# Three sets of operand buffers that change roles, a reordered outer sum and a third small buffer in an attention and feed-forward kernel

## The chip, the cores and the metric

The kernel runs on one core of a Trainium2 chip. The metric is the device time in microseconds of one execution. A core has a matrix engine (TensorE, PE in the profile; PEld is its loading of weights), a vector engine (VectorE, DVE), a scalar engine (ScalarE, ACT), a general engine (GpSimd, POOL) and a queue that starts transfers (SyncE, SP). Each works through its own list of instructions in order and waits on semaphores for the others.

## The reference

The input has 8 batches of 512 rows of 512 numbers, all in float32. The first part is an attention layer with low-rank projections and rotary positions. The second part, which the change is about, is a feed-forward layer with Hadamard transforms:

```python
x = x + _layernorm(attention(_layernorm(x)))        # first part
h = _layernorm(x)
h = fwht(h * SU_ug) / 64                            # transform over 512
up   = h @ W_up.T   * (Wscale_ug[:2048] * 64)       # 512 -> 2048
gate = h @ W_gate.T * (Wscale_ug[2048:] * 64)
g = silu(gate) * up
g = fwht(g * SU_dp) / 64                            # transform over 2048
y = g @ W_down.T * (Wscale_dp * 64)                 # 2048 -> 512
x = x + _layernorm(y)
```

The second transform is folded into `W_down` beforehand, on the chip.

## The kernel before

**Two stages.** The attention stage takes the first 900 us or so. The feed-forward stage takes the 8 batches in four pairs (p = 0 to 3); batches 2p and 2p + 1 are pair p. Each pair runs 8 blocks (i = 0 to 7); a block makes 128 of the 2048 inner columns twice over, i and i + 8, for both batches, for gate and up.

**Seven products instead of eight.** The four quarters of weights (i and i + 8, two halves of the 512 inputs) and the four quarters of the transformed input (two batches, two halves) are multiplied as a 2 by 2 block product in a Strassen-like form: seven products, numbered and ordered by `ORDER = (1, 2, 6, 5, 7, 3, 4)`. Products 1, 2 and 3 use quarters of the input as they are (B11, B21, B22). Products 5, 6, 7 and 4 use T1, T2, T3 and T4, which VectorE makes by four subtractions in `operand` (L230): T1 = B12 - B11, T2 = B22 - T1, T3 = B22 - B12, T4 = B21 - T2.

**First half** (pair 0). `seven` (L1153) runs the seven products for gate and then for up of each block; a pass over one of them is a unit, u = 0 to 15. During the units the layer's inputs of the next pair are brought in by `in_step` (L177): `in_flip` transposes 128 rows on TensorE and VectorE writes `xflat` (L197); `in_had` multiplies it with a Hadamard matrix (L204), and copies (L209) and adds (L210 to L214) write it to the pair's input tile `xb[b]`. `FIRST_CUTS` says how many steps a unit takes: none to two, all in `middle`, after product 3. `hook(n)` is called after product n and, in the last unit, makes operands for pair 1.

**Second half** (pairs 1 to 3). The same scheme is used once more inside each product: gate and up, and the two halves of the product's operand, make a second 2 by 2 product, so `deep` (L1102) makes each of the seven products out of seven small ones, 128 x 256 matmuls (L1112) into one of four PSUM banks. Their operands are three subtractions each, `tt` (`deep_operand`, L1005), and one in place (`deep_last`, L1010). What follows one product's small ones:

```python
nc.scalar.copy(m1, small(1))                    # L1119 ACT
nc.vector.tensor_add(gate[:, :HS], small(2), m1)    # L1120
nc.vector.tensor_add(u2, small(6), m1)          # L1122
nc.scalar.copy(m5, small(5))                    # L1123 ACT
nc.vector.tensor_add(u3, small(7), u2)          # L1126
nc.gpsimd.tensor_add(up[:, HS:], u3, m5)        # L1127
nc.vector.tensor_add(gate[:, HS:], small(3), u2)    # L1128
nc.gpsimd.tensor_add(gate[:, HS:], gate[:, HS:], m5)    # L1129
nc.vector.tensor_add(up[:, :HS], small(4), u3)  # L1131
```

`m1` and `u2` are halves of one tile, `m5` and `u3` of another; four tiles of the tag "sig" go round, so each kind has two. `gate` and `up` are halves of a `pr` tile; six `pr` tiles go round. `pair` (L1325) then lets GpSimd combine the seven `pr` tiles (L1334, two instructions for each sum), ScalarE applies silu (L1151) and VectorE scales (L1147), and the result `g` goes into the down-projection's queue.

**What orders the work.** The order is written out by hand. `place(n, at)` is called inside product n at at = 1, 2, 3, and there the queue's down-projection matmuls (L1212), the norms and stores of finished batches, and the operands of the next pair are put in. `prepare` (L1287) has a table with keys (i, n, at): "T" makes a T, "tt" one of a product's three subtractions, "last" the one in place. For the next pair it starts in block NH - 2 = 6 of the pair before and ends in block 0 of the pair itself.

**Buffers of the operands.** Input tiles `xb[b]` of all pairs go round in two buffers of tag kT and two of tag qT. T1 to T4 of all pairs lie in the two tiles of `home`. The weights of the last batch's down-projection (`wd_load_last`, L1078) take new tiles of the tags kT, qT and xT.

Of the kernel before, what the change touches and what calls it, by code (L numbers as in the profile page):

```python
# [33 lines left out]
def sandwich_kernel(  # L34
# [164 lines left out]
    def in_had(j):  # L199
        b, t = rows[j]  # L200
        if t == 0:
            xb[b] = qkv.tile([P, NK, S], F32, tag=("kT", "qT")[b % 2], name=f"xb_{b}")
        ps = room["bank"](f"fxh_{j}").rearrange("p (k q) -> p k q", k=NK)
        nc.tensor.matmul(ps, lhsT=h128, rhs=xflat[j], start=True, stop=True)  # L204
        z, a = room["z"](f"xz_{j}"), room["a"](f"xa_{j}")
        pv_ = ps.rearrange("p (a t) q -> p a t q", t=2)
        zv = z.rearrange("p (a t) q -> p a t q", t=2)[:, :, 1, :]
        av = a.rearrange("p (a t) q -> p a t q", t=2)
        nc.scalar.copy(zv, pv_[:, :, 1, :])  # L209
        nc.vector.tensor_add(av[:, :, 0, :], pv_[:, :, 0, :], zv)  # L210
        nc.vector.tensor_sub(av[:, :, 1, :], pv_[:, :, 0, :], zv)
        d = xb[b][:, :, ts(t, P)]
        nc.gpsimd.tensor_add(d[:, 0:2, :], a[:, 0:2, :], a[:, 2:4, :])
        nc.gpsimd.tensor_sub(d[:, 2:4, :], a[:, 0:2, :], a[:, 2:4, :])  # L214
# [4 lines left out]
    def operand(p, k):  # L219

        b11, b21 = xb[2 * p][:, 0:2], xb[2 * p][:, 2:4]
        b12, b22 = xb[2 * p + 1][:, 0:2], xb[2 * p + 1][:, 2:4]
        if k == 0:
            ops[p] = {"B11": b11, "B21": b21, "B22": b22}
        o = ops[p]
        if p == 0 and k < 2:
            home.append(qkv.tile([P, NT, D], F32, tag="v", name=f"T{k + 1}"))
        o[f"T{k + 1}"] = home[k % 2][:, 2 * (k // 2) : 2 * (k // 2) + 2]
        a, b = [(b12, b11), (b22, o.get("T1")), (b22, b12), (b21, o.get("T2"))][k]
        nc.vector.tensor_sub(o[f"T{k + 1}"], a, b)  # L230

# [846 lines left out]
    def wd_load_last():  # L1078
        n = len(wd_last)
        if n % 4 == 0:  # L1080
            pool, tag = [(qkv, "kT"), (qkv, "qT"), (xt_p, "xT"), (xt_p, "xT")][n // 4]
            wd_home.append(pool.tile([P, NT, D], F32, tag=tag, name=f"wdl_{n // 4}"))
        wd_last.append(wd_home[-1][:, n % 4])
        nc.sync.dma_start(out=wd_last[n], in_=wdd[:, ts(order_of(NB - 1)[n], D)])

# [7 lines left out]
    def product(p, i, what, n):  # L1093
# [5 lines left out]
            )  # L1099
        return ps  # L1100

    def deep(p, i, n, gate, up, copied, place):  # L1102

        x_, t, w = ops[p][OPERAND[n]], tt[p, n], wq.pop((p, i, n))
        rhs = {
            1: x_[:, 0, :HS], 2: x_[:, 1, :HS], 6: t[:, 1], 5: t[:, 0],
            7: x_[:, 0, HS:], 3: x_[:, 1, HS:], 4: t[:, 2],
        }

        def small(m):  # L1110
            ps = ubank(f"d{n}{m}_{p}_{i}")[:, :HS]
            nc.tensor.matmul(ps, lhsT=w[:, INNER[m]], rhs=rhs[m], start=True, stop=True)  # L1112
            return ps

        one, two = (
            fs.tile([P, 2, HS], F32, tag="sig", name=f"d{k}{n}_{p}_{i}", bufs=4) for k in "ab"
        )
        m1, u2, m5, u3 = one[:, 0], one[:, 1], two[:, 0], two[:, 1]
        nc.scalar.copy(m1, small(1))  # L1119
        nc.vector.tensor_add(gate[:, :HS], small(2), m1)  # L1120
        place(1)
        nc.vector.tensor_add(u2, small(6), m1)  # L1122
        nc.scalar.copy(m5, small(5))  # L1123
        copied()
        place(2)
# [4 lines that stand above are left out]
        place(3)  # L1130
        nc.vector.tensor_add(up[:, :HS], small(4), u3)  # L1131
# [155 lines left out]
    def prepare(p, i, n, at):  # L1287
        q = p + 1 if i >= NH - 2 else p
        if q >= NP or q == 0:
            return  # L1290
        todo = {
            (NH - 2, 1, 2): [("ops",), ("tt", 1, 0)], (NH - 2, 1, 3): [("tt", 1, 1)],
            (NH - 2, 2, 3): [("tt", 1, 2)], (NH - 2, 3, 1): [("tt", 2, 0)],
            (NH - 2, 3, 2): [("tt", 2, 1)], (NH - 2, 3, 3): [("tt", 2, 2)],
            (NH - 1, 7, 2): [("T", 0)], (NH - 1, 7, 3): [("T", 1)], (NH - 1, 3, 1): [("last", 1)],
            (NH - 1, 3, 2): [("T", 2)], (NH - 1, 4, 1): [("tt", 6, 0)],
            (NH - 1, 4, 2): [("tt", 6, 1)], (NH - 1, 4, 3): [("tt", 6, 2)],
            (0, 1, 1): [("T", 3)], (0, 1, 2): [("last", 2)], (0, 1, 3): [("last", 6)],
            (0, 2, 1): [("tt", 5, 0)], (0, 2, 3): [("tt", 5, 1)], (0, 6, 1): [("tt", 5, 2)],
            (0, 6, 2): [("last", 5), ("tt", 7, 0)], (0, 5, 1): [("tt", 7, 1)],  # L1300
            (0, 5, 2): [("tt", 7, 2)], (0, 5, 3): [("last", 7)], (0, 7, 1): [("tt", 3, 0)],
            (0, 7, 2): [("tt", 3, 1)], (0, 7, 3): [("tt", 3, 2)], (0, 3, 1): [("last", 3)],
            (0, 3, 2): [("tt", 4, 0)], (0, 3, 3): [("tt", 4, 1)], (0, 4, 1): [("tt", 4, 2)],
            (0, 4, 2): [("last", 4)],
        }
        for kind in todo.get((i, n, at), ()):
            make(q, *kind)
# [12 lines left out]


    PARTS = {1: (1, 3), 2: (1, 3), 6: (1, 2, 3), 5: (1, 3), 7: (1, 3), 3: (1, 2, 3), 4: (1, 3)}
    rest_of = {}

    def pair(p, i, inputs):  # L1325

        bA, bB = 2 * p, 2 * p + 1
        pr = {}
        before = dict(rest_of)
        rest_of.clear()  # L1330

# [56 lines left out]
        for n in ORDER:  # L1388
# [4 lines left out]
            if n in (2, 5, 3):  # L1393
                if inputs:
                    step(n, *inputs.pop(0))
            pr[n] = pr_tile(f"pr{n}_{p}_{i}")
            deep(
                p, i, n, pr[n][:, 0], pr[n][:, 1], lambda n=n: copied(n), lambda at, n=n: place(n, at)
            )
            if n == 2 and i == 0:  # L1400
                add(2, 2, 1)
            elif n == 6:
                add(6, 6, 1)
            elif n == 7:
                add(7, 7, 6)
                add(6, 6, 5)
                add(5, 5, 7)
            elif n == 3:
                add(3, 3, 6)
            elif n == 4:  # L1410
                add(4, 4, 7)
        rest_of.update(c22=(pr[5], bB, i + NH), c12=(pr[3], bB, i), c21=(pr[4], bA, i + NH))

# [5 lines left out]
    for u, (p, i, what) in enumerate(units):  # L1421
# [24 lines left out]
        def hook(n):  # L1446
            if sums and n != 1:
                sums.pop(0)()
            if u == 2 and n in (1, 2):
                in_stats(first + n - 1)  # L1450
            if u == 2 * NH - 1:
                for kind in {
                    1: [("ops",), ("tt", 1)], 2: [("tt", 2)], 5: [("T", 0)], 7: [("T", 1), ("last", 1)],
                    3: [("T", 2)], 4: [("tt", 6)],
                }[n]:
                    make(1, *kind)

        seven(p, i, what, filler, middle, hook)
        if u == 1:
# [129 lines left out]
```

## Time and profile before

| what | us |
|---|---|
| median of three runs | 2120.41 |
| the three runs | 2116.99, 2121.7, 2120.41 |
| the profiled execution's own time | 2117.1 |
| its span | 2115.3 |
| TensorE busy in it | 2081.0 |
| GpSimd busy | 1573.5 |
| VectorE busy | 1408.2 |
| ScalarE busy | 745.3 |

The profile is of one execution. Busy times overlap, since the engines work side by side. The granted clock of TensorE was 0.998 of full speed over the span. A line of a groups view has the source line, the engine, the operation and its tiles, the count, the busy time and the mean of one in ns, and after the last bar how long the engine had been idle just before these instructions and who ended that. In tile names `d` is a small product's PSUM bank, `da` and `db` are the tiles of m1, u2 and of m5, u3.

### The profile page before, as it was taken

The numbers are of one execution on the slowest core, as the hardware profiler recorded it, in microseconds if no ns is written. First come the engines' busy times: TensorE is split into PE (matmuls) and PEld (weight loads), VectorE is DVE, ScalarE is ACT, GpSimd is POOL, SyncE is SP. The second block draws the span as 40 slices with busy tenths as digits, with TensorE's granted clock in tenths as the row PEclk, the third lists the DMA queues.
The fourth block names the chain that finished last, engine by engine and source line by source line (L and its number), as shares of the span: only waits on it lengthen the run. The fifth ranks groups of instructions, "written<-read, shape, count | busy, mean of one in ns | idle before, by whom it ended". The sixth has DMA issues, their size and how long they took to land.

```text
span 2115.3 us, 26783 instructions
## 1 busy us (share of the span) xinstructions
PE 2081.0 (98%) x9042; PEld 1057.5 (50%) x9042; DVE 1408.2 (67%) x2356; ACT 745.3 (35%) x1199; POOL 1573.5 (74%) x1629
## 2 busy tenths in 40 slices
PE   8999999999999999999999999999999999999998
PEld 4333333333333333344444677676676776777753
DVE  5697777676767678365545865768766668656542
ACT  3454545455555555522221122222122221222211
POOL 4787979797878788655443679788888879787762
PEclk9999999999999999999999999999999999999999
DMA  3111121212111123236455343434344344444331
GB/s 124 33 31 51 46 56 42 61 41 48 54 46 51 31 61 81 89 118 187 151 177 163 124 138 130 156 131 142 122 141 144 127 137 142 137 152 140 132 117 70
DMA packets 215913, 218.12 MB, mean 103 GB/s; under 512 B 87376, under 2 KB 147920, under 8 KB 215776
## 3 DMA queue, kind: packets, MB, share of 16 engines
q1 hardware_dynamic: 215424, 215.32, 32.5%
q8 instruction: 72, 1.18, 0.2%
q0 software_dynamic: 352, 1.08, 0.1%
q14 instruction: 65, 0.53, 0.1%
HBM read 169.18 MB, written 46.92 MB: 102 GB/s over the span
## 4 chain that ended last, share of the span: by engine, by line
PE 90%; DVE 4%; POOL 3%; issue 1%; ACT 1%; DMA 1%; SPq 0%; POOLq 0%; DVEq 0%; ACTq 0%
PE d L1112 22%; PE psy L1212 17%; PE s L520 6%; PE ops L599 6%; PE ps_k L432 5%; PE ps_y L655 5%; PE t L566 5%; PE u L1097 4%; PE g L1097 4%; PE t L557 3%; PE psz L1490 2%; PE l L616 2%; POOL pr L1334 2%; PE ps_q L447 1%; PE ps_v L459 1%; PE ps_cq L400 1%
## 5 line engine op out<-in xcount | busy, mean ns | idle before, releaser
L1212 PE MATMUL psy<-wd,g 128*128 128x512 f32 x896 | 449.3, 593 | 0.0
L528 DVE TENSOR_REDUCE nm<-s 128x2 f32<-128x1024 f32 x256 | 300.7, 1216 | 174.0 <-PE s L520 173.9
L1334 POOL TENSOR_TENSOR pr<-pr,pr 128x512 f32<-128x512 f32 x294 | 381.1, 1324 | 7.4
L587 POOL TENSOR_TENSOR p<-p,p 128x512 f32<-128x512 f32 x244 | 329.6, 1381 | 22.1 <-PE ops L599 22.1
L578 ACT ACTIVATE p<-t 128x1024 f32<-128x1024 f32 x256 | 251.8, 1023 | 89.0 <-PE t L566 89.0
L1112 PEld LDWEIGHTS d<-tt,wq 128*128 128x128 f32 x864 | 164.5, 191 | 144.8 <-issue 105.7
L1112 PE MATMUL d<-tt,wq 128*128 128x256 f32 x864 | 234.7, 380 | 0.1
L1127 POOL TENSOR_TENSOR pr<-db 128x256 f32<-128x256 f32 x168 | 132.2, 787 | 115.7 <-DVE db L1126 104.2
L1112 PE MATMUL d<-T,wq 128*128 128x256 f32 x768 | 199.4, 381 | 9.1 <-DVE T L1010 4.9
L1212 PEld LDWEIGHTS psy<-wd,g 128*128 128x128 f32 x896 | 169.8, 190 | 49.3 <-issue 29.4
L1112 PE MATMUL d<-xb,wq 128*128 128x256 f32 x720 | 183.6, 380 | 2.4 <-DVE xb L1010 1.8
L1123 ACT COPY db<-d 128x256 f32<-128x256 f32 x168 | 62.7, 373 | 323.5 <-PE d L1112 266.1
L1119 ACT COPY da<-d 128x256 f32<-128x256 f32 x168 | 62.6, 373 | 299.5 <-PE d L1112 219.0
L1112 PEld LDWEIGHTS d<-T,wq 128*128 128x128 f32 x768 | 144.8, 191 | 46.4 <-issue 15.5
L1112 PEld LDWEIGHTS d<-xb,wq 128*128 128x128 f32 x720 | 135.3, 190 | 56.8 <-issue 31.9
L520 PE MATMUL s<-kT,qT 32*128 32x512 f32 x1024 | 153.8, 639 | 0.7 <-DVE nm L528 0.7
L566 PE MATMUL t<-qT,kT 32*128 32x512 f32 x1024 | 142.8, 598 | 0.0
L1129 POOL TENSOR_TENSOR pr<-pr,db 128x256 f32<-128x256 f32 x168 | 137.4, 818 | 0.0
L599 PE MATMUL ops<-p,v 128*32 128x512 f32 x1024 | 136.8, 605 | 0.0
L1131 DVE TENSOR_TENSOR pr<-d,db 128x256 f32<-128x256 f32 x168 | 70.5, 419 | 74.4 <-PE d L1112 73.9
L432 PE MATMUL ps_k<-xT,wkr_sb 128*128 128x512 f32 x256 | 118.3, 605 | 0.7 <-ACT xT L390 0.7
L655 PE MATMUL ps_y<-wo_sb,oT 128*128 128x512 f32 x256 | 115.8, 593 | 0.6 <-DVE oT L650 0.6
(206 smaller groups left out, 3236.2 us busy)
## 6 DMA issues: line engine op xcount, KB each, us to landing
wq<-wdeep SPq DMA_DIRECT2D x168, 448.0 KB, 4.1
wd<-wdd SPq DMA_DIRECT2D x112, 256.0 KB, 2.7
wdeep<-w SPq DMA_DIRECT2D x32, 448.0 KB, 5.8
xr<-in_x SPq DMA_DIRECT2D x32, 256.0 KB, 2.7
xin<-x1d SPq DMA_DIRECT2D x32, 256.0 KB, 3.3
xres<-x1d SPq DMA_DIRECT2D x32, 256.0 KB, 3.1
out<-fy SPq DMA_DIRECT2D x32, 256.0 KB, 2.0
rec<-rd SPq DMA_DIRECT2D x124, 64.0 KB, 2.0
```

What stands on the lines that cost most here:

```text
L432: nc.tensor.matmul(ps, lhsT=wkr_sb[:, k, ts(g, P)], rhs=xT[b][:, k, :], start=(k == 0), stop=(k == NK - 1),)
L520: nc.tensor.matmul(sp[j // 2][:, j % 2, :], lhsT=qT[b][rows, g, ts(qc, P)], rhs=kT[b][rows, g, :], start=True, stop=True,)
L528: nc.vector.tensor_reduce(nms[n][:, qc, 2 * h : 2 * h + 2], sp[h], AX.X, ALU.max, negate=True)
L566: nc.tensor.matmul(sp[j // 2][:, j % 2, :], lhsT=kT[b][rows, g, ts(c, P)], rhs=qT[b][rows, g, :], start=False, stop=True,)
L578: nc.scalar.activation(pt[n, c, h], sp[h], AF.Exp)
L587: nc.gpsimd.tensor_add(into, into, pt[n, c, j // 2][:, j % 2, :])
L599: nc.tensor.matmul(o_ps[n][j * DH : (j + 1) * DH, :], lhsT=vv[b][:, c, ds(g * P + j * DH, DH)], rhs=pt[n, c, j // 2][:, j % 2, :], start=( ...
L655: nc.tensor.matmul(ps, lhsT=oT[b][:, k, ts(qc, P)], rhs=wo_sb[:, k, :], start=False, stop=(k == NK - 1),)
L1097: nc.tensor.matmul(ps, lhsT=w[:, SLOT[n], k, :], rhs=rhs[:, k, :], start=k == 0, stop=k == 1)
L1112: nc.tensor.matmul(ps, lhsT=w[:, INNER[m]], rhs=rhs[m], start=True, stop=True)
L1212: nc.tensor.matmul(ys_[t], lhsT=g[:, ts(t, P)], rhs=w, start=n == 0, stop=n == NI - 1)
L1334: nc.gpsimd.tensor_add(pr[n][:, h], pr[a][:, h], pr[b][:, h])
```

## The change

1. `in_had`: pairs 2 and 3 get no new input tiles. Pair 2's inputs go into the two `home` tiles, pair 3's into `xb[0]` and `xb[1]`.
2. `operand`: pair 0 keeps its T in `home`. Pair p writes T1 to T4 over the quarters B11, B21, B22 and B12 of pair p - 1. So three sets of two tiles change roles as inputs and T. The last batch's first eight weight blocks go into `xb[2]` and `xb[3]`.
3. `prepare` and the last two units' `hook`: operands are made in another order and mostly one or more products earlier; in the last block of a pair tt5, the in-place step of 5 and one part of tt7 join.
4. `deep`: one tile for m1 and u2, and three that take turns for m5 and u3.
5. `pair`: six fixed `pr` tiles that change roles from block to block, and another order of the outer sums: one after product 5, two after product 7 (before: three after 7).
6. In the first half, a unit with two input steps does the first after product 5.

```diff
     def in_had(j):
         b, t = rows[j]
         if t == 0:
-            xb[b] = qkv.tile([P, NK, S], F32, tag=("kT", "qT")[b % 2], name=f"xb_{b}")
+            if b < 4:
+                xb[b] = qkv.tile([P, NK, S], F32, tag=("kT", "qT")[b % 2], name=f"xb_{b}")
+            else:
+                xb[b] = home[b - 4] if b < 6 else xb[b - 6]
...
-        o[f"T{k + 1}"] = home[k % 2][:, 2 * (k // 2) : 2 * (k // 2) + 2]
+        if p == 0:
+            o[f"T{k + 1}"] = home[k % 2][:, 2 * (k // 2) : 2 * (k // 2) + 2]
+        else:
+            b, half = [(0, 0), (0, 1), (1, 1), (1, 0)][k]
+            o[f"T{k + 1}"] = xb[2 * p - 2 + b][:, 2 * half : 2 * half + 2]
...
-            wd_home.append(pool.tile([P, NT, D], F32, tag=tag, name=f"wdl_{n // 4}"))
+            wd_home.append(
+                xb[2 + n // 4] if n < 8 else pool.tile([P, NT, D], F32, tag=tag, name=f"wdl_{n // 4}")
+            )
...
+    inner = []
+
     def deep(p, i, n, gate, up, copied, place):
...
-        one, two = (
-            fs.tile([P, 2, HS], F32, tag="sig", name=f"d{k}{n}_{p}_{i}", bufs=4) for k in "ab"
-        )
-        m1, u2, m5, u3 = one[:, 0], one[:, 1], two[:, 0], two[:, 1]
+        if not inner:
+            inner.extend(
+                fs.tile([P, 2, HS], F32, tag="sig", name=f"inner{k}", bufs=4) for k in range(4)
+            )
+        turn = stream.index((p, i, n)) % 3
+        m1, u2, m5, u3 = inner[0][:, 0], inner[0][:, 1], inner[1 + turn][:, 0], inner[1 + turn][:, 1]
...
-            (NH - 1, 7, 2): [("T", 0)], (NH - 1, 7, 3): [("T", 1)], (NH - 1, 3, 1): [("last", 1)],
-            (NH - 1, 3, 2): [("T", 2)], (NH - 1, 4, 1): [("tt", 6, 0)],
-            (NH - 1, 4, 2): [("tt", 6, 1)], (NH - 1, 4, 3): [("tt", 6, 2)],
+            (NH - 1, 2, 1): [("T", 0)], (NH - 1, 2, 3): [("last", 1)], (NH - 1, 5, 2): [("T", 1)],
+            (NH - 1, 5, 3): [("tt", 5, 0)], (NH - 1, 7, 2): [("tt", 5, 1)],
+            (NH - 1, 7, 3): [("tt", 5, 2)], (NH - 1, 3, 1): [("tt", 6, 0)],
+            (NH - 1, 3, 2): [("tt", 6, 1)], (NH - 1, 3, 3): [("tt", 6, 2)],
+            (NH - 1, 4, 1): [("T", 2)], (NH - 1, 4, 2): [("last", 5)], (NH - 1, 4, 3): [("tt", 7, 0)],
             (0, 1, 1): [("T", 3)], (0, 1, 2): [("last", 2)], (0, 1, 3): [("last", 6)],
-            (0, 2, 1): [("tt", 5, 0)], (0, 2, 3): [("tt", 5, 1)], (0, 6, 1): [("tt", 5, 2)],
-            (0, 6, 2): [("last", 5), ("tt", 7, 0)], (0, 5, 1): [("tt", 7, 1)],
-            (0, 5, 2): [("tt", 7, 2)], (0, 5, 3): [("last", 7)], (0, 7, 1): [("tt", 3, 0)],
-            (0, 7, 2): [("tt", 3, 1)], (0, 7, 3): [("tt", 3, 2)], (0, 3, 1): [("last", 3)],
-            (0, 3, 2): [("tt", 4, 0)], (0, 3, 3): [("tt", 4, 1)], (0, 4, 1): [("tt", 4, 2)],
-            (0, 4, 2): [("last", 4)],
+            (0, 2, 1): [("tt", 7, 1)], (0, 2, 3): [("tt", 7, 2)], (0, 6, 1): [("last", 7)],
+            (0, 6, 2): [("tt", 3, 0)], (0, 5, 2): [("tt", 3, 1)], (0, 5, 3): [("tt", 3, 2)],
+            (0, 7, 2): [("last", 3)], (0, 7, 3): [("tt", 4, 0)], (0, 3, 1): [("tt", 4, 1)],
+            (0, 3, 2): [("tt", 4, 2)], (0, 3, 3): [("last", 4)],
...
-            pr[n] = pr_tile(f"pr{n}_{p}_{i}")
+            if n == 1:
+                new = (
+                    dict(zip((1, 2, 6, 5, 7, 3), (pr[k] for k in (2, 5, 6, 7, 3, 4))))
+                    if pr
+                    else {k: pr_tile(f"pr{k}") for k in (1, 2, 6, 5, 7, 3)}
+                )
+            pr[n] = new.get(n, new[1])
...
+            elif n == 5:
+                add(5, 5, 6)
             elif n == 7:
-                add(7, 7, 6)
-                add(6, 6, 5)
-                add(5, 5, 7)
+                add(6, 6, 7)
+                add(7, 7, 5)
             elif n == 3:
-                add(3, 3, 6)
+                add(3, 3, 5)
             elif n == 4:
-                add(4, 4, 7)
-        rest_of.update(c22=(pr[5], bB, i + NH), c12=(pr[3], bB, i), c21=(pr[4], bA, i + NH))
+                add(4, 4, 6)
+        rest_of.update(c22=(pr[7], bB, i + NH), c12=(pr[3], bB, i), c21=(pr[4], bA, i + NH))
...
             if u == 2 * NH - 1:
                 for kind in {
-                    1: [("ops",), ("tt", 1)], 2: [("tt", 2)], 5: [("T", 0)], 7: [("T", 1), ("last", 1)],
-                    3: [("T", 2)], 4: [("tt", 6)],
+                    1: [("T", 0)], 2: [("last", 1), ("T", 1)], 5: [("tt", 5)], 7: [("tt", 6)],
+                    3: [("last", 5), ("T", 2)], 4: [("tt", 7, 0)],
                 }[n]:
                     make(1, *kind)
+            if u == 2 * NH - 2 and n in (1, 4):
+                if n == 1:
+                    make(1, "ops")
+                make(1, "tt", 1 + n // 4)
+            if n == 5 and len(steps) > 1:
+                in_step(*steps.pop(0))
```

Each block still has the same number of sums, copies and small products.

## The prediction

> **What bounds the kernel now.** I read the page's head first, then the second half block by block in the windows view, then the waits and the timeline inside the blocks that are too long.
>
> ```profile
> span 2115.3 us, 26783 instructions
> PE 2081.0 (98%) x9042; PEld 1057.5 (50%) x9042; DVE 1408.2 (67%) x2356; ACT 745.3 (35%) x1199; POOL 1573.5 (74%) x1629
> ```
>
> TensorE (PE) is busy 98% of the span, and this change takes no matmul away. Only time in which TensorE idles (34 us in all, start and end included) or crawls can be won. Where is it? The next view cuts the second half at the ScalarE copies of L1119 for product 1, so that each stretch is one block (p, i). Columns: length, busy time of PE, PEld, DVE, ACT, POOL with counts, clock, DMA.
>
> ```profile
> 1169.36:1207.46 38.10, 35.61 (x131) 24.37 (x130) 35.20 (x70) 5.84 (x15) 24.64 (x24) 1.00 0.35 117
> 1427.30:1462.19 34.89, 34.89 (x131) 24.70 (x130) 27.15 (x48) 9.13 (x21) 28.80 (x27) 1.00 0.40 139
> 1462.19:1502.27 40.08, 34.89 (x121) 22.83 (x120) 33.52 (x65) 7.79 (x18) 38.84 (x34) 0.96 0.34 119
> 1756.85:1796.95 40.10, 36.14 (x131) 24.19 (x130) 33.77 (x65) 7.70 (x18) 38.87 (x34) 1.00 0.45 151
> 1796.95:1831.84 34.89, 34.89 (x131) 24.70 (x130) 20.94 (x47) 7.71 (x18) 24.45 (x27) 1.00 0.42 139
> ```
>
> An undisturbed block takes 34.89 us with PE busy throughout: pair 1's last (second line) and pair 3's second (fifth). The three first blocks, where a pair's operands are still being made, take 38.10, 40.08 and 40.10: 3.2, 5.2 and 5.2 us too long. In them GpSimd (POOL) is busy 38.8 of 40.1 us and VectorE (DVE) 33.5. Pair 2's first block also holds less work, as the down-projection's matmuls alone show:
>
> ```profile
> 1427.30:1462.19 34.89, 16.34 (x32) 6.08 (x32) 1.00 0.40 139
> 1462.19:1502.27 40.08, 11.68 (x22) 4.18 (x22) 0.96 0.34 119
> ```
>
> Ten rows at 0.43 us (start to start in the timeline) are missing (products 6 and 5 have no down-projection work), so its content is 30.6 us and it loses 9.5. Who is late? First what PE waits for in pair 3's first block, then VectorE's groups there.
>
> ```profile
> PE d L1112 <- DVE T L1010: 1.4, 1, 1.4
> PE d L1112 <- DVE xb L1010: 1.3, 1, 1.3
> PE d L1112 <- ACT db L1123: 1.0, 1, 1.0
> ```
>
> ```profile
> L1120 DVE TENSOR_TENSOR pr<-d,da 128x256 f32<-128x256 f32 x7 | 3.0, 423 | 2.4 <-POOL pr L1334 1.7 <-PE d L1112 0.4 <-ACT da L1119 0.4
> L1126 DVE TENSOR_TENSOR db<-d,da 128x256 f32<-128x256 f32 x7 | 2.9, 417 | 2.2 <-POOL pr L1129 1.2 <-PE d L1112 0.9
> ```
>
> Two causes, then: operands written just in time (L1010), and buffers that GpSimd gives back late (L1129 for m5 and u3, L1334 for the products). The timeline shows each, and a third one in the first half:
>
> ```profile
> 999.02 1.10 PE L204 MATMUL fxh<-xflat,h 128*128 128x512 f32 x2 [1.11 <-DVE xflat L197]
> ...
> 1470.56 1.16 POOL L1129 TENSOR_TENSOR pr<-pr,db 128x256 f32<-128x256 f32 x1
> 1471.76 0.37 ACT L1123 COPY db<-d 128x256 f32<-128x256 f32 x1 [4.45 <-POOL pr L1129]
> ...
> 1784.76 8.23 POOL L1334 TENSOR_TENSOR pr<-pr,pr 128x512 f32<-128x512 f32 x6
> 1786.14 1.45 DVE L1010 TENSOR_TENSOR xb<-xb 128x256 f32<-128x256 f32 x1
> 1787.74 1.10 PE L1112 MATMUL d<-xb,wq 128*128 128x256 f32 x4 [1.28 <-DVE xb L1010]
> ```
>
> At 999 a Hadamard matmul stands right behind its transpose and waits 1.11 us for xflat. At 1471.76 the m5 copy starts as soon as GpSimd lets go. At 1786.14 operand 3's last subtraction, made during product 3 itself, is stretched to 1.45 us beside GpSimd's six outer sums, and PE stands.
>
> **What the Trainium skill says.** "Perfetto Trace Analysis", Identifying the Most-Contended Engine: matmul busy time is a poor measure of distance to the limit. Agreed here: pair 2's first block shows 34.89 us busy for 30.6 of content. "GPSIMD Engine Reference", Key points: GpSimd shares its SBUF interfaces with VectorE, with contention from VectorE instructions with two SBUF inputs. Agreed: tt<-T (L1005) means 412 ns in pair 1's first block, 1016 in pair 2's. "TensorE: Matmul & The Clock Gate", What's actually happening: after about 3.4 us of idleness the clock is halved. The 0.96 above is 1.6 us lost in 40.08, in the block with the thinnest PE work; no single wait there is that long, so I read it as low activity.
>
> **The change, part by part.**
>
> *Input step after product 5 (first half).* Units with two steps ran them back to back. Where the transpose comes first (two units) PE waited 2.2 us in all (L204's group). Now two products stand between: **-2.2**. Where the Hadamard step comes first it moves ahead of products 7, 3 and 4: a 0.37 us copy on ACT, two 0.42 on DVE, and two adds of 0.9 and 0.7 that get ahead of L1183 and L1186 on POOL. POOL idles 55 us before eight L1183, so 0; uncovered, 1.6 each in two units.
>
> *Operands earlier.* A pair's last block has 3 L230 (5.04 us), 1 L1010 (0.97) and 3 L1005 (2.94). The new table puts 3, 2 and 7 there: 4 x 0.98 + 0.97 = 4.9 us more, so DVE goes from 27.15 to 32.0 of 34.89. By product the worst are 2 and 5: five own instructions at a pitch of 0.33 (1.65), a scale at 1.22, a T at 1.9, one more at 1.0: 5.8 us against a PE time of 4.74. Product 7 before holds two T and a scale, 6.7 us, and PE didn't stop, so 0; at worst 1 us for each of products 2, 5 and 4 in two blocks, 6 in all. The first block loses 4 L1005 (0.83) and 1 L1010 (0.74), 4.1 us. T's new homes are halves whose readers (product 1, 2 or 3 of the old pair) are past: no wait but one for PE's product 1 in the first half's last unit, where VectorE needs product 2 next anyway.
>
> What is late next in the first blocks? VectorE by product, with a scale at 0.92, fy at 0.69, T4 at 1.26: product 1 4.4, product 2 4.2, 6 4.1, 5 4.2, 7 5.5, 3 5.4, 4 2.5 us. PE: 4.74, 4.74, 5.6, 4.74, 4.74, 5.6, 4.74. The larger of each sums to 35.7 us for pair 3. In pair 2, PE has 3.0 for products 6 and 5, so VectorE sets them: 33.6, and I add 0.9 for the thin stretch and its clock, 34.5.
>
> *Third buffer for m5 and u3.* ScalarE's m5 copy waits for GpSimd three products back, not two: some 5 us more. The wait at 1471.76 cost PE 1.0 us. I went through GpSimd's row in pair 2's first block with its own durations: it is past product 3's two adds by 1463, 4's by 1469, 1's by 1473.5, 2's by 1475, and they are wanted by products 2, 6, 5 and 7 at 1469, 1474, 1478 and 1482. These waits end. In return m1 and u2 have one buffer instead of two: 0 here, see the third rival.
>
> *Outer sums.* Still 12 instructions of 1.3 us a block, but four in a row after product 7, not six (5.5 us, not 8.23): GpSimd is 2.7 us less behind when the next pair begins, enough for L1120's 1.7. Product 6 takes a buffer whose last reader is the sum after product 4, two products before, as product 2's was and is; 0, at worst another 1.7 in two blocks.
>
> *Other homes of xb and of the last weights.* The homes are free half a pair ahead. Eight loads on SP now wait for T's readers (products 5 and 6 before them), with wq loads queued behind, which are issued two ahead: 0, at worst one landing of 4.1.
>
> **Sum.** First half -2.2; pair 1's first block 38.1 to 35.5, -2.6; pair 2's 40.1 to 34.5, -5.6; pair 3's 40.1 to 35.6, -4.5. Together **-14.9**, on the profiled run's 2117.1 us: 2102.2. The median of the runs, 2120.41, stands 3.3 above it: **2105.5**.
>
> **Rivals.** *VectorE stays the limit* in the first blocks: the moved subtractions are stretched beside GpSimd, and only the waits on GpSimd (1.7 + 1.2 us in each of two blocks) and the first half's 2.2 go: -8.0, 2112.4. For it: VectorE already runs 33.5 us there. Against: it loses 4.1. *No net effect*: what the first blocks win, the last blocks lose (6 us), and GpSimd's new tight buffers and the SP wait (3.4 + 4.1) take the rest, about -1.4: 2119. Against: each would have to reach its worst. *Slower, by the one m1 buffer*: each of 168 products' m1 copy must wait until VectorE has read the m1 (and, if the tile counts whole, the u2) before. If it comes late PE stops, for four PSUM banks hold little. Before 1462.19 that last read ends at 1461.33, 0.86 us ahead. From 0.115 us a product on (19.3 us in all) the kernel is slower by over 0.2%; at 0.2 it is 33.6 - 14.9 = 19 us slower, 2139. Against: 0.86 is ample wherever PE sets the pace. The change not doing what it says is no case: the instructions and homes follow from the tables.
>
> **Chances.** Main case 0.62, its own range 2101 to 2109 (20.1 us, all losses gone, would be 2100.3); VectorE limit 0.20; no net effect 0.08; slower 0.10. Faster by over 0.2% (4.2 us, about what a measurement of this kernel tells from no change): 0.82; within: 0.08; slower: 0.10. The range 2101 to 2117 leaves out the slower case, most of the third and a small tail, about 0.18.
>
> **What would show it.** Right: first blocks of 34 to 36 us between L1119's copies; no PE wait on L1010; no ACT or DVE wait on POOL's L1129; no 1.11 us gaps before L204; last blocks still 34.9. Wrong: last blocks of 36 or more (operands moved too much), copies of m1 that wait for VectorE in every block (the one buffer), or first blocks near 38 with VectorE busy throughout.

## The result, and the profile after

The changed kernel takes **2102.06 us** (median of four runs, 2101.41 to 2104.13) against 2119.61 for the kernel before in the same comparison (four runs, 2116.99 to 2121.70). The ratio is 0.992, with a 95% interval from 0.9902 to 0.9937: faster by 0.6 to 1.0%. The forecast was 2105.5, within 2101 to 2117.

The profiled execution of the changed kernel took 2102.66 us, 14.44 less than the profiled one of before (2117.1). The head of its page:

```profile
span 2100.9 us, 26741 instructions
PE 2076.8 (99%) x9035; PEld 1057.4 (50%) x9042; DVE 1414.4 (67%) x2356; ACT 745.3 (35%) x1199; POOL 1575.4 (75%) x1629
```

TensorE's busy time fell by 4.2 us, the span by 14.4. Most of what went was idleness. VectorE and GpSimd run as many instructions as before, and VectorE is busy 6.2 us longer. The next view cuts the changed kernel at the copies of m1 (L1132, before L1119). The stretches are pair 1's first block, pair 1's last, pair 2's first, pair 3's first and pair 3's second; the columns are those of the prediction's second fence.

```profile
1168.18:1203.07 34.89, 34.89 (x131) 24.61 (x130) 30.53 (x63) 5.84 (x16) 25.04 (x24) 1.00 0.39 128
1422.89:1458.14 35.25, 35.15 (x131) 24.61 (x130) 28.82 (x52) 9.12 (x21) 29.43 (x27) 1.00 0.40 138
1458.14:1492.70 34.56, 32.65 (x121) 21.96 (x120) 33.48 (x61) 7.80 (x19) 34.01 (x31) 1.00 0.39 137
1747.64:1783.36 35.72, 35.55 (x131) 24.44 (x130) 33.14 (x61) 7.71 (x19) 35.17 (x32) 1.00 0.51 169
1783.36:1818.24 34.88, 34.88 (x131) 24.70 (x130) 21.10 (x47) 7.70 (x18) 28.20 (x30) 1.00 0.44 141
```

The three first blocks have come down from 38.10, 40.08 and 40.10 to 34.89, 34.56 and 35.72. Part of pair 2's gain is clock: 0.96 in that block before, 1.00 now, which is 1.6 of its 40.08 us. Pair 1's is now as long as an undisturbed block, with TensorE busy in all of it. Pair 2's is the shortest and yet the worst: its down-projection has still only 22 matmuls, as the same stretch shows for that line (L1225, before L1212) alone.

```profile
1458.14:1492.70 34.56, 11.23 (x22) 4.18 (x22) 1.00 0.39 137
```

Against the content of 30.6 us that the prediction worked out, it loses 4.0. TensorE's waits in that stretch show on whom:

```profile
PE d L1123 <- DVE inner L1139: 1.4, 2, 0.7
PE d L1123 <- DVE pr L1144: 0.2, 1, 0.2
```

VectorE's own sums of the small products (L1139, L1144), and no longer a just-made operand, are what TensorE waits for. These waits make 1.6 of the 4.0 us; the rest lies in time that the profile counts as busy. In pair 3's first block the waits view lists no wait of TensorE. The groups of VectorE there answer to L1120 and L1126 of before:

```profile
L1133 DVE TENSOR_TENSOR pr<-d,inner 128x256 f32<-128x256 f32 x7 | 2.9, 412 | 0.5 <-PE d L1123 0.5
L1139 DVE TENSOR_TENSOR inner<-d,inner 128x256 f32<-128x256 f32 x7 | 2.9, 413 | 0.6 <-PE d L1123 0.6
```

The idle time before them had 1.7 and 1.2 us that ended with GpSimd; now all of it ends with TensorE. In the first half, the group of Hadamard matmuls (L207, before L204) in the stretch from 940 to 1160 has no idle time before it, where it had 2.2 us behind VectorE's `xflat`:

```profile
L207 PE MATMUL fxh<-xflat,h 128*128 128x512 f32 x16 | 8.2, 592 | 0.0
```

Where the 14.4 us lie, stretch by stretch between the same instructions of the two profiled executions:

| stretch | before | after | difference | predicted |
|---|---|---|---|---|
| attention, to the first gate matmul | 914.83 | 916.33 | +1.5 | 0 |
| first half, to pair 1's first m1 copy | 254.53 | 251.85 | -2.7 | -2.2 |
| first block of pair 1 | 38.10 | 34.89 | -3.2 | -2.6 |
| first block of pair 2 | 40.08 | 34.56 | -5.5 | -5.6 |
| first block of pair 3 | 40.10 | 35.72 | -4.4 | -4.5 |
| last blocks of pairs 1 and 2 | 69.8 | 70.5 | +0.7 | 0 |
| blocks between | | | 0.0 | 0 |
| from pair 3's second block on | 318.35 | 317.54 | -0.8 | 0 |
| sum | | | -14.4 | -14.9 |

The attention's +1.5 is mostly a wait of 1.4 us for a normalized input, in a part that the change leaves as it was. It is no effect of the change: the profiled execution of the kernel before has no such wait, and ten of the twelve experiments' have one, of 0.5 to 1.7 us. Nor is the -0.8 at the end: over all fourteen profiled executions that stretch takes 317.2 to 318.7 us, with the homes of before as with the new ones. The last blocks' loss is 0.36 us between the m1 copies of products 7 and 3 (5.10 us for 4.74). Just before it, in product 5, the new table puts T2 behind a scale (VectorE's timeline in pair 1's last block; start, duration):

```profile
1438.81 1.35 DVE L1160 SCALAR_TENSOR_TENSOR g<-pr,wsu 128x512 f32<-128x512 f32 x1
1440.42 1.96 DVE L237 TENSOR_TENSOR xb<-T,xb 128x1024 f32<-128x1024 f32 x1
```

T2 ends at 1442.38, 0.3 us before product 7's copy, and VectorE's sums of product 5 stand behind it. hold_t, below, takes T2 out of this place.

### The profile page after: what moved, and what is told of

It is laid out like the page before. It is cut to its first block, busy times and chain, and to the rows that moved or that the text cites. A ratio compares the mean times of both kernels' runs of the same rounds, so it can differ in the third digit from the quotient of the medians.

```text
span 2100.9 us, 26741 instructions
## 1 busy us (share of the span) xinstructions
PE 2076.8 (99%) x9035; PEld 1057.4 (50%) x9042; DVE 1414.4 (67%) x2356; ACT 745.3 (35%) x1199; POOL 1575.4 (75%) x1629
## 4 chain that ended last, share of the span: by engine, by line
PE 94%; DVE 3%; issue 1%; POOL 1%; ACT 1%; DMA 0%; SPq 0%; POOLq 0%; DVEq 0%; ACTq 0%
PE d L1123 24%; PE psy L1225 18%; PE s L527 6%; PE ops L606 6%; PE ps_k L439 5%; PE ps_y L662 5%; PE t L573 5%; PE u L1106 5%; PE g L1106 4%; PE psz L1516 3%; PE t L564 3%; PE l L623 2%; PE ps_q L454 2%; PE ps_v L466 1%; PE ps_cq L407 1%; PE fxh L207 1%
## 5 line engine op out<-in xcount | busy, mean ns | idle before, releaser
L1225 PE MATMUL psy<-wd,g 128*128 128x512 f32 x896 | 448.9, 592 | 0.0
L1347 POOL TENSOR_TENSOR pr<-pr,pr 128x512 f32<-128x512 f32 x294 | 391.6, 1357 | 9.0
L1123 PE MATMUL d<-xb,wq 128*128 128x256 f32 x992 | 254.2, 380 | 1.9 <-DVE inner L1139 1.4
L1140 POOL TENSOR_TENSOR pr<-inner 128x256 f32<-128x256 f32 x168 | 126.0, 750 | 138.5 <-DVE inner L1139 105.9
L1123 PEld LDWEIGHTS d<-xb,wq 128*128 128x128 f32 x992 | 186.7, 190 | 62.4 <-issue 30.1
L1225 PEld LDWEIGHTS psy<-wd,g 128*128 128x128 f32 x896 | 169.7, 190 | 49.3 <-issue 29.4
L1136 ACT COPY inner<-d 128x256 f32<-128x256 f32 x168 | 62.6, 373 | 309.6 <-PE d L1123 291.5
L1132 ACT COPY inner<-d 128x256 f32<-128x256 f32 x168 | 62.6, 372 | 300.3 <-PE d L1123 193.2
L1142 POOL TENSOR_TENSOR pr<-pr,inner 128x256 f32<-128x256 f32 x168 | 136.5, 813 | 0.0
L1123 PE MATMUL d<-T,wq 128*128 128x256 f32 x496 | 127.6, 380 | 0.2
L1144 DVE TENSOR_TENSOR pr<-d,inner 128x256 f32<-128x256 f32 x168 | 70.5, 420 | 75.5 <-PE d L1123 72.9
L1135 DVE TENSOR_TENSOR inner<-d,inner 128x256 f32<-128x256 f32 x168 | 70.5, 419 | 62.4 <-PE d L1123 62.0
```

The lines of the kernel that those rows point to most:

```text
L1225: nc.tensor.matmul(ys_[t], lhsT=g[:, ts(t, P)], rhs=w, start=n == 0, stop=n == NI - 1)
L1347: nc.gpsimd.tensor_add(pr[n][:, h], pr[a][:, h], pr[b][:, h])
```

## The experiments

The theory: the gain is that of the operands' earlier places, and buffers and sums alone bring nothing. The rival: GpSimd's late buffers were the limit, and the third m5 turn and the new sums freed them. In the diffs, lines with a minus are those of the kernel named first. "First" and "last" blocks are stretches between m1 copies of the profiled execution, as above.

### The table of operands

**old_table**: the changed kernel with before's table and `hook`; T3 stands one product later than before, since its new home is read until then.

```diff
-            (NH - 1, 2, 1): [("T", 0)], (NH - 1, 2, 3): [("last", 1)], (NH - 1, 5, 2): [("T", 1)],
...
+            (NH - 1, 7, 2): [("T", 0)], (NH - 1, 7, 3): [("T", 1)], (NH - 1, 3, 1): [("last", 1)],
+            (NH - 1, 4, 1): [("T", 2), ("tt", 6, 0)],
...
```

> The changed kernel with the operand table of before (T3 one product later, since its new home is still read in product 3) and the last unit's hook of before; buffers, sums and input steps stay changed. Theory A (two causes that add up: operands just in time, and buffers that GpSimd returns late): the PE waits on L1017 (in-place subtraction) come back, about 3 us in each of the three first blocks, which take 38, 37.5 and 38.5 us instead of 34.9, 34.6 and 35.7; in all +9 us, 2111. Theory B (the operands' early place carries the whole gain, the buffers nothing): first blocks of 38, 40 and 40, +12 to +13 us, 2115. Theory C (the buffers carry it): under +3 us.

Measured: 2117.61 (20 runs) against 2120.04, ratio 0.9986 (0.9979 to 0.9993). Its last block of pair 1 and first block of pair 3:

```profile
1427.06:1462.03 34.97, 34.88 (x130) 24.20 (x128) 25.29 (x46) 9.12 (x21) 29.22 (x27) 1.00 0.41 139
1755.95:1798.45 42.50, 37.85 (x131) 25.61 (x132) 37.52 (x67) 7.70 (x18) 38.81 (x35) 0.96 0.42 143
```

First blocks are 38.35, 39.26 and 42.50 us. The last is longer than before's 40.10, though buffers and sums are the new ones and, of VectorE and ScalarE, only one m5 copy still waits for GpSimd (1.8 us). About 1.7 of its 2.4 us more are clock (0.96 for 1.00, last section). VectorE is busy 37.52 us in it, and TensorE waits for late operands again:

```profile
PE d L1123 <- DVE T L1017: 2.0, 1, 2.0
PE d L1123 <- DVE xb L1017: 1.3, 1, 1.3
```

The kernel is slower than even theory B had it (2115). What is left of the gain, 0.14%, is about what the input step gives alone (step_only, below).

**table_only**: the changed kernel with two m5 turns and before's sums and `pr` tiles, so that homes, table and input step alone are new.

```diff
-        turn = stream.index((p, i, n)) % 3
+        turn = stream.index((p, i, n)) % 2
...
-            elif n == 5:
-                add(5, 5, 6)
             elif n == 7:
-                add(6, 6, 7)
-                add(7, 7, 5)
+                add(7, 7, 6)
+                add(6, 6, 5)
+                add(5, 5, 7)
...
```

> The changed kernel with two turns for m5 and the old outer sums together, so that of the second half only the operands' homes and table are new. Theory A: all GpSimd waits of before come back (1.0 us of PE at product 2, VectorE's 1.7 and 1.2): +3 us in each of pair 2's and pair 3's first blocks, pair 1's unchanged, +6 in all, 2108. Theory B: under +1 us, 2102 to 2103. If the two buffers replace each other, this run is slower than two_m5 and old_sums added up.

Measured: 2105.41, ratio 0.9928 (0.9914 to 0.9943). First blocks 34.88, 34.72 and 35.49, as in the changed kernel; last blocks 36.18 and 36.17. The waits on GpSimd are back in them, as VectorE's in pair 3's first block shows, where L1347 is before's L1334:

```profile
DVE pr L1133 <- POOL pr L1347: 1.9, 1, 1.9
```

TensorE waits for nothing there all the same. So the table, with its homes and the input step, carries all of the first blocks' gain and 14.6 us of the whole (2120.04 less 2105.41; the step alone is 3.3 of them), where the changed kernel has 17.5.

**step_only**: the kernel before with the input step after product 5.

```diff
+            if n == 5 and len(steps) > 1:
+                in_step(*steps.pop(0))
```

> The kernel before with the first half's input step after product 5 alone. All theories: the two waits of 1.11 us ahead of the Hadamard matmul go, the first half is 2.2 to 2.7 us shorter, the three first blocks stay 38.1, 40.1 and 40.1; about 2117.5 against 2120.0 of before on this chip.

Measured: 2116.37 (19 runs) against 2119.68, ratio 0.9982 (0.9976 to 0.9989): 3.3 us (2.3 to 5.1 by the interval) for the predicted 2.2. The second half's first blocks are before's (39.79, 40.08 and 40.10; the first has a stretch of slow clock, shown at the end).

### The small buffers and the sums

**two_m5**: the changed kernel with two m5 turns.

```diff
-        turn = stream.index((p, i, n)) % 3
+        turn = stream.index((p, i, n)) % 2
```

> The changed kernel with two turns instead of three for the tile of m5 and u3 (one of the four tiles stays unused). Theory A: ScalarE's m5 copy of product 2 waits for GpSimd again, 1 us of PE in pair 2's and pair 3's first blocks: 35.6 and 36.7 us, +2 us in all. Theory B: once the sums are reordered GpSimd is past product 4's adds before product 2 wants the tile, so the third turn is spare: first blocks unchanged within 0.3 us, 2102. My reading of the changed kernel's timeline (product 1's adds end at 1469.8, product 6's copy starts at 1469.77) is for B with at most 0.5 us.

Measured: 2102.65, ratio 0.9915 (0.99 to 0.993). First blocks 34.89, 34.56 and 35.72, last 35.23: the third turn is spare.

**m5_only**: the kernel before with the four fixed small tiles (one m1, three m5).

```diff
-        m1, u2, m5, u3 = one[:, 0], one[:, 1], two[:, 0], two[:, 1]
...
+        turn = stream.index((p, i, n)) % 3
+        m1, u2, m5, u3 = inner[0][:, 0], inner[0][:, 1], inner[1 + turn][:, 0], inner[1 + turn][:, 1]
```

> The kernel before with the four fixed small tiles alone: one for m1 and u2, three in turn for m5 and u3. As in the prediction: ScalarE's wait on GpSimd at product 2 (1.0 us of PE in pair 2's and pair 3's first blocks) goes and nothing else: -2 us, 2117.7 against before. Theory B (VectorE's late operands set those blocks): the blocks stay 40 us, the saved wait turning into a later one on VectorE: 2119.7. The one m1 tile as a cost: blocks in mid-pair longer than 34.89 us.

Measured: 2119.65 (12 runs) against 2119.50, ratio 1.0003 (0.9994 to 1.0012). First blocks 39.97 (with a stretch of slow clock that before's 38.10 lacks), 40.04 and 40.05. The wait it was meant to end has ended: before, ScalarE's m5 copies waited 10.4 us for L1129 in pair 3's first block, and here ScalarE waits for GpSimd not at all. VectorE's waits in that block (L1124 is before's L1120, L1338 its L1334):

```profile
DVE pr L1124 <- POOL pr L1338: 3.6, 2, 2.1
```

They were 1.7 us for the same sums and 1.2 for L1129. The stall for the m5 copy has become a longer one, one buffer further on, for the outer sums. And TensorE's two waits for operands, in the same block, are what they were, 1.4 and 1.3:

```profile
PE d L1114 <- DVE T L1010: 1.4, 1, 1.4
PE d L1114 <- DVE xb L1010: 1.3, 1, 1.3
```

**sums_only**: the kernel before with the new order of the sums.

```diff
+            elif n == 5:
+                add(5, 5, 6)
             elif n == 7:
-                add(7, 7, 6)
-                add(6, 6, 5)
-                add(5, 5, 7)
+                add(6, 6, 7)
+                add(7, 7, 5)
...
```

> The kernel before with the new order of the outer sums alone. As in the prediction: VectorE's wait for the sum after product 3 (1.7 us) goes in two first blocks and GpSimd is 2.7 us less behind: -1 to -2 us. Theory B: the first blocks stay within 0.5 us of 40.1.

Measured: 2118.75 (12 runs), ratio 0.9997 (0.9989 to 1.0006). Pair 3's first block is longer than before's 40.10, most of it by the clock (0.96, about 1.7 us), and VectorE's waits there are on TensorE and ScalarE alone:

```profile
1758.07:1800.20 42.13, 37.82 (x131) 25.14 (x130) 37.57 (x66) 7.69 (x18) 38.88 (x35) 0.96 0.42 144
```

Read DVE against before's 33.77 (x65): one instruction more in the stretch, and 3.8 us more of busy time. VectorE no longer stands for GpSimd; it runs beside it, and its instructions take longer. Two of its groups, of before and then of sums_only:

```profile
L1147 DVE SCALAR_TENSOR_TENSOR g<-pr,wsu 128x512 f32<-128x512 f32 x4 | 3.7, 924 | 0.0
L1010 DVE TENSOR_TENSOR T<-T 128x256 f32<-128x256 f32 x4 | 2.4, 605 | 0.0
```

```profile
L1147 DVE SCALAR_TENSOR_TENSOR g<-pr,wsu 128x512 f32<-128x512 f32 x4 | 4.5, 1131 | 0.0
L1010 DVE TENSOR_TENSOR T<-T 128x256 f32<-128x256 f32 x4 | 3.4, 846 | 0.0
```

Its sums with an input in PSUM (L1120 to L1131) stay at 0.41 us each. TensorE waits there 2.0 us for `T` and 1.3 for `xb`, before 1.4 and 1.3.

**m5_sums**: both edits together.

> The kernel before with both: four fixed small tiles and the new order of the sums. Sum of the prediction's terms: both first blocks 2 to 3 us shorter, -4 to -6 us. Theory B: all waits on GpSimd gone, and the first blocks still 39 to 40 us, under -2 us in all.

Measured: 2118.43 (12 runs), ratio 0.9995 (0.9987 to 1.0004). First blocks 38.35, 38.77 and 42.13. In none of the three does VectorE or ScalarE wait for GpSimd, and TensorE still waits for operands in pair 3's:

```profile
PE d L1114 <- DVE T L1010: 2.0, 1, 2.0
PE d L1114 <- DVE xb L1010: 1.3, 1, 1.3
```

Pair 3's block has the slow clock (0.96), pair 2's is free of it (1.00, before 0.96), so the two changes of length are about those of the clock. With every wait on GpSimd that the prediction named gone at once, the kernel isn't measurably faster; by the interval it gains 2.8 us at most. This is the rival's case, and it falls.

**old_sums**: the changed kernel with before's sums and `pr` tiles.

> The changed kernel with the outer sums in the old order (three after product 7) and six pr tiles that go round as before. Theory A: GpSimd is 2.7 us later at a pair's start, VectorE's first write of product 2 waits about 1.7 us for the sum after product 3 again, and PE loses about half of that: +1 us in each of two first blocks, +2 in all, with the third m5 tile keeping the copies free. Theory B: within 0.5 us of the changed kernel, 2102.

Measured: 2104.45, ratio 0.9924 (0.9909 to 0.9939). First blocks 34.88, 34.59 and 35.03; last 36.28 and 36.15. The windows line of pair 1's last block, and then a wait of VectorE in it:

```profile
1421.81:1458.09 36.28, 35.42 (x131) 24.48 (x130) 31.73 (x52) 9.13 (x20) 30.31 (x27) 1.00 0.39 134
```

```profile
DVE pr L1375 <- POOL pr L1142: 0.6, 1, 0.6
```

In the changed kernel's 35.25 this wait isn't there. The sum that VectorE makes itself (L1375) stands in product 6 for GpSimd's part of product 2, and product 6 takes 6.37 us instead of 5.60. That this wait is the cause is argued from its place. It isn't enough alone: crowd, below, has one of 0.8 us there, with less made before it, and its product 6 takes 5.59. So the new sums are worth about 1 us in each of two last blocks, and only where these are as full as the new table makes them. They cost something too: with before's sums pair 3's first block takes 35.03 instead of 35.72, and with before's table the new sums lengthen pair 1's last block (35.26 in sums_only, for 34.89). Against two_m5, in the same comparison, the whole is 1.8 us.

### Is the room to spread needed?

**crowd**: the kernel before with the input step and, of the new table, the first block (for pair 1 the last units' `hook`); the same operands are made in the last block, but in the homes of before, which come free only from product 5 on, so within products 7, 3 and 4. Buffers and sums are before's.

```diff
+            (NH - 1, 7, 1): [("T", 0)], (NH - 1, 7, 2): [("T", 1)],
+            (NH - 1, 7, 3): [("last", 1), ("tt", 5, 0)], (NH - 1, 3, 1): [("tt", 5, 1)],
+            (NH - 1, 3, 2): [("tt", 5, 2), ("T", 2)], (NH - 1, 3, 3): [("tt", 6, 0)],
+            (NH - 1, 4, 1): [("tt", 6, 1)], (NH - 1, 4, 2): [("tt", 6, 2), ("last", 5)],
+            (NH - 1, 4, 3): [("tt", 7, 0)],
...
```

> The kernel before with its old homes, buffers and sums, and the input step; the operand table makes in each last block exactly what the changed table makes there, but squeezed into products 7, 3 and 4, as early as the old homes of T allow; first blocks use the changed table. If only the amount moved out of the first blocks counts (theory B), first blocks 34.9 to 36 and a last block under 36.5: about 2105. If the new homes earn their place because they let the work spread over products 2 to 4 (theory D): VectorE has 20.6 us in three products of 15.1 us, a last block grows by 2 to 4 us in pairs 1 and 2, and the kernel is at 2108 to 2112.

Measured: 2107.07, ratio 0.9939 (0.9924 to 0.9953). Its last block of pair 1 and first of pair 3:

```profile
1423.07:1459.40 36.33, 35.26 (x130) 24.16 (x128) 29.04 (x49) 9.12 (x21) 30.21 (x28) 1.00 0.38 134
1750.03:1786.24 36.21, 35.45 (x131) 24.91 (x132) 32.86 (x64) 7.70 (x18) 34.12 (x31) 1.00 0.49 166
```

No new buffer is in this kernel, and it has most of the gain, 12.6 us (3.3 of them the step's). By the medians it is 1.7 us slower than table_only, with intervals that overlap; in the profiles the two differ most in pair 1's first block (36.27 for 34.88) and pair 3's (36.21 for 35.49). The three sets of homes are a refinement, then: the decisive step is that the operands are made earlier.

Read VectorE's column against before's 33.77 (x65) in pair 3's first block: 32.86 (x64) here, and 33.14 (x61) in the changed kernel. Fewer of its instructions there make operands by subtraction (tt and in place: 18 before, 15 here, 14 in the changed kernel), but others take longer, and crowd enters the block with two sums still to make. So its block is 3.9 us shorter with only 0.9 us less of VectorE's work in it, and TensorE waits for no operand there. How much is owed to the work that left the block, and how much to the earlier order of what stayed, no run separates.

### What is still lost

**hold**: the changed kernel; five parts of the down-projection, two matmuls each, stay in the queue in block 3 of pair 1. Pair 2's first block then has 32 of them and not 22.

```diff
-            if at in PARTS[n]:
+            if at in PARTS[n] and not (p == 1 and i == 3 and at == 3 and n != 4 and n != 1):
```

> The changed kernel, with five of the down-projection's parts left in the queue in block 3 of pair 1, so that they run in products 6 and 5 of pair 2's first block, where PE has none. If VectorE sets that block (34.6 us for 30.6 us of PE work), the parts fit beside it: block 3 of pair 1 shrinks by 4.3 us, pair 2's first block grows to 35 to 36, net -2.5 to -3.5 us, 2099. If PE were the limit there, the block would grow by the full 4.3 us and the time stay at 2102.

Measured: 2097.86 against 2119.68, ratio 0.9895 (0.9879 to 0.9912). The block that gave, and the one that got:

```profile
1277.38:1309.71 32.33, 32.33 (x131) 23.98 (x130) 22.50 (x50) 10.17 (x22) 28.61 (x31) 1.00 0.46 159
1454.36:1490.13 35.77, 35.57 (x131) 24.47 (x130) 33.22 (x61) 7.70 (x19) 35.22 (x32) 1.00 0.41 140
```

The giver went from 36.62 to 32.33, ten matmuls of 0.43 us; the taker from 34.56 to 35.77. So 3.1 of the 4.0 us that pair 2's first block lost to VectorE were time in which TensorE could have worked.

**hold_t**: as hold, with T2 in product 6 and not in product 5.

```diff
-            (NH - 1, 2, 1): [("T", 0)], (NH - 1, 2, 3): [("last", 1)], (NH - 1, 5, 2): [("T", 1)],
+            (NH - 1, 2, 1): [("T", 0)], (NH - 1, 2, 3): [("last", 1)], (NH - 1, 6, 3): [("T", 1)],
```

> As hold, and T2 made in product 6 of the last block (place 3) instead of product 5 (place 2), where the scale and T2 together delay PE by 0.36 us. If that wait is VectorE's load in product 5, the two last blocks are back to 34.9: 0.7 us less than hold. If T2's 1.9 us only move the wait to product 6, no gain.

Measured: **2096.91** (2096.29 to 2097.16), ratio 0.9891 (0.9876 to 0.9906), the fastest of all medians here. Pair 1's last block, and pair 2's first:

```profile
1417.66:1452.55 34.89, 34.89 (x131) 24.72 (x130) 29.08 (x52) 9.12 (x21) 30.61 (x27) 1.00 0.42 139
1452.55:1487.93 35.38, 35.28 (x131) 24.56 (x130) 32.59 (x61) 7.69 (x19) 34.83 (x32) 1.00 0.42 142
```

The last block's 0.36 us is won back, and 0.4 in the first block with it. First blocks are now 34.89, 35.38 and 35.39; an undisturbed one takes 34.89.

**hold_u**: as hold_t, with the subtractions for products 3 and 4 one place earlier in the first block.

```diff
-            (0, 6, 2): [("tt", 3, 0)], (0, 5, 2): [("tt", 3, 1)], (0, 5, 3): [("tt", 3, 2)],
-            (0, 7, 2): [("last", 3)], (0, 7, 3): [("tt", 4, 0)], (0, 3, 1): [("tt", 4, 1)],
+            (0, 6, 2): [("tt", 3, 0)], (0, 6, 3): [("tt", 3, 1)], (0, 5, 2): [("tt", 3, 2)],
+            (0, 5, 3): [("last", 3)], (0, 7, 2): [("tt", 4, 0)], (0, 7, 3): [("tt", 4, 1)],
```

> As hold_t (parts held back, T2 in product 6), with operand 3's second subtraction and in-place step, and operand 4's first two, one place earlier in the first block, so that product 3 has one VectorE instruction less. Product 3 took 5.96 us there for 5.60 of PE work, and product 4 4.82 for 4.74. If VectorE's load in products 7 and 3 is the cause: pair 2's and pair 3's first blocks 35.0 instead of 35.4, -0.8 us against hold_t, about 2096. If GpSimd's four sums beside them stretch whatever stands there: no gain.

Measured: 2097.28 (2095.90 to 2099.48), ratio 0.9897 (0.9882 to 0.9912): no gain over hold_t. First blocks 34.88, 35.33 and 35.31. From m1 copy to m1 copy in pair 2's first block, product 3 fell from 5.97 to 5.55 us, and products 5 and 7 rose from 4.74 and 4.79 to 4.96 and 5.01: the delay only changes its place.

## Why the prediction was right, and where its reasons were not

**First blocks, -2.6, -5.6 and -4.5: right in the cause and in the sums, in part by luck.** They measured -3.2, -5.5 and -4.4. That VectorE would still set pair 2's first block, with its thin down-projection, is what the waits on L1139 and L1144 show; hold shows it again, by filling it. But product by product, between the m1 copies, the blocks differ from the list (in us, products in their order):

| | 1 | 2 | 6 | 5 | 7 | 3 | 4 | sum |
|---|---|---|---|---|---|---|---|---|
| pair 3, the larger of each | 4.74 | 4.74 | 5.6 | 4.74 | 5.5 | 5.6 | 4.74 | 35.7 |
| pair 3, measured | 4.74 | 5.08 | 5.60 | 4.74 | 4.79 | 5.96 | 4.81 | 35.72 |
| pair 2, the larger of each | 4.74 | 4.74 | 4.1 | 4.2 | 5.5 | 5.6 | 4.74 | 33.6 |
| pair 2, measured | 4.74 | 5.08 | 3.73 | 3.50 | 5.88 | 6.01 | 5.62 | 34.56 |

The 0.8 us that the list put into product 7 of pair 3 came in products 2 and 3; the part in product 2 is T2's delay passed on, for hold_t, which moves T2, has 4.74 there. In pair 2, products 6 and 5 ran faster than the list has them, and the time was paid later, in 7, 3 and 4. The 0.9 us added there "for the thin stretch and its clock" filled the gap, though the block's clock was 1.00. Pair 1's 35.5 had no list; the block took 34.89.

VectorE was to have 4.1 us less to do in each. Its busy time fell by 4.7 us in pair 1's, by 0.6 in pair 3's and by nothing in pair 2's, since what stayed took longer: in pair 3's the four scales 1.15 us each for 0.92, the in-place steps 0.98 for 0.75. So the first rival's premise, that the subtractions stretch, came true in two blocks. Its conclusion, that VectorE stays the limit in all three and about 8 us are all there is, fell: pair 1's block is full and pair 3's nearly so.

The reading behind it, GpSimd busy 38.8 of 40.1 us, holds for two of the blocks only. In pair 1's it was busy 24.64 of 38.10 and the waits view lists no wait on it; of that block's 3.2 us, 2.2 were one wait of TensorE for an operand.

**Third buffer, "these waits end": they end, and it is worth nothing.** The step put the wait at 1471.76 down as 1.0 us of TensorE's. m5_only takes that wait away, alone, and the kernel stays where it was, since VectorE then waits 3.6 us for the sums. In the changed kernel two turns do as well as three. The sum wasn't harmed only because the step was worked into the blocks' total and not added to it.

**Outer sums, "2.7 us less behind, enough for L1120's 1.7": right on the wait, wrong on its worth.** sums_only ends that wait and gains nothing measurable, and m5_sums ends both. What they freed VectorE spent in longer instructions. The sums do pay in the changed kernel, but not by the wait that they were priced for: 1 us in each last block (old_sums).

**Last blocks, 0, at worst 6: 0.7 in all.** The step named product 5 and its T behind a scale at 5.8 us against 4.74, and chose zero, because product 7 of before held more and TensorE had not stopped. The scale took 1.35 and the T 1.96, near the estimates of 1.22 and 1.9, and 0.36 us was lost in each of the two blocks, one product later than the step had it. The precedent should have been worth less than the sum.

**One m1 buffer, the slower rival: excluded.** The blocks between first and last have the same lengths in both kernels (36.62 to 36.62 for block 3 of pair 1 in m5_only too), so a product pays nothing for it; the rival needed 0.115 us.

**No net effect, the rival in which every cost reaches its worst: excluded.** Its 6 us in the last blocks were 0.7; VectorE waits for GpSimd in none of the changed kernel's first blocks; and no wait of TensorE for the last weights shows after pair 3's first block, where before has one of 0.5 us.

**First half, -2.2: -2.7 in the profile, and 3.3 by the medians of step_only.** step_only's profile has 251.85 us for it, as the changed kernel's, so all of the 2.7 is the step's. Where the part beyond the two waits lies is open.

**From the sum to the median: the term that missed most.** The sum gave 2102.2 for an execution like the profiled one, and the profiled one took 2102.66. The 3.3 us that the median of before stood above its own profiled execution were then added, and they didn't carry over: the changed kernel's median stands 0.6 below its profiled execution. The 3.3 came from three runs; with the fourth that median is 2119.61 and the offset 2.5. The profiled execution of before was near the fastest of the four. The clock has a part in it, too, as the last section shows.

## What to carry to other kernels

When an engine's waits for buffers and its late operands are seen in one block, undo them one at a time before giving either a price: here every wait on buffers could go and the time stayed, because the same engine then spent the time in longer instructions and the operands came as late as before. Making the operands earlier, some of them in the block before, where that engine has room, was what paid, and a crude version of it without any new buffers had most of the gain. A block that holds less work for the bounding engine than its neighbours is a place to move that work to, and a difference between one profiled execution and a median is no constant to carry from one kernel to the next.

## What the runs showed of the hardware

TensorE's granted clock falls to half for about 3.4 us at a time, in some executions and not in others. One such stretch in pair 2's first block of the kernel before, by the windows view:

```profile
1483.80:1487.20 3.40, 3.40 (x8) 2.35 (x7) 2.63 (x5) 0.23 (x1) 3.40 (x4) 0.50 0.15 59
```

In step_only it comes in pair 1's first block, whose clock there is 0.68 over 5 us right after a wait of 2.2 us for an operand:

```profile
1203.00:1208.00 5.00, 5.00 (x13) 3.24 (x14) 1.42 (x4) 0.37 (x1) 4.84 (x7) 0.68 0.08 16
```

The kernel before has the same wait of 2.2 us in that block with a clock of 1.00. The Trainium skill, "TensorE: Matmul & The Clock Gate", What's actually happening, has the clock halved after about 3.4 us of idleness; here it halved after waits of 1.5 to 2.2 us, and not every time. Half speed for 3.4 us costs 1.7.

The change takes these stretches away. Of the profiled executions, the six of kernels with before's table have one or two each in a first block (before, old_table, step_only and m5_sums one; m5_only and sums_only two); the eight with the new table's places, crowd among them, have none there. In the 76 executions of the kernel before that were timed beside the experiments, the time follows the clock: a median of 2118.06 us where the mean clock was 0.999 (12 executions), 2119.41 at 0.998 (35), 2121.17 at 0.997 (24) and 2122.55 at 0.996 (5). The changed kernel's four had 0.999 three times and 0.998 once. So the clock goes some way to explain that the medians differ by 17.5 us and the profiled executions by 14.4; how much of the 3.1 us, no run shows.

The second is how far VectorE's subtractions stretch. In the stretch around pair 1's first block of before, seven with both inputs in SBUF (128 x 256, L1005 and L1010) ran while GpSimd had no instruction under way, and each took 0.40 to 0.42 us; eight ran wholly beside GpSimd's instructions and took 0.68 to 1.49. Around pair 3's, where GpSimd hardly pauses, those beside it took 0.41 to 1.49. In sums_only VectorE's busy time in a block rose by 3.8 us with one instruction more, while its sums with an input in PSUM stayed at 0.41.
